# A four-layer gated transformer on one core: the order of VectorE and ScalarE in the first expert stage, single top-k rounds, ternary weights in three parts

## The chip, the core and the metric

The kernel runs on one core of a Trainium2 chip. A core has a matrix engine (TensorE), a vector engine (VectorE), a scalar engine with activation functions (ScalarE), a general engine (GpSimd), and SyncE, which here only issues transfers. Each engine executes its own instructions in program order and waits on semaphores for the others. Operands lie in SBUF (128 partitions); matrix products land in PSUM, eight banks of 128 x 512 fp32. The metric is device time in microseconds (us) of one execution; lower is better.

## The reference

The input x has 4 sequences of 256 tokens of width 256 (1024 tokens, eight tiles of 128). Four layers follow, each an attention-like block over a context `ctx` (4 x 256 x 64) and a feed-forward block, each added to x with a gate. What matters here:

```python
# layer 0: softmax of a normalized similarity, then a dense mixture of experts
x = x + tanh(g_xattn[0]) * L0_attention(layernorm(x), ctx)
logits = xn @ gate_w + gate_b;  top_idx = top_k(logits, 2)
all_out = relu(einsum('nsd,edo->nseo', xn, expert_w) + expert_b)   # 8 experts
x = x + tanh(g_ffn[0]) * take(all_out, top_idx).mean(axis=2)
# layer 1: causal attention with 16 heads, then a ternary feed-forward block
x = x + tanh(g_xattn[1]) * L1_attention(layernorm(x), ctx)
wq = clip(round(w / mean|w|), -1, 1) * mean|w|      # for w_gate, w_up, w_down
x = x + tanh(g_ffn[1]) * h_bitlinear(silu(bitlinear(xn, w_gate)) * bitlinear(xn, w_up), w_down)
# layer 2: a graph of ctx alone: rows of sim keep their 76 largest entries
sim = scores(ctx, ctx);  thr = top_k(sim, 76)[..., -1:]
A = sigmoid(sim) * (sim >= thr);  A = (A + A.T) / 2
```

Layers 2 and 3 end with routed experts. The graph A depends on ctx only and is needed first after layer 1.

## The kernel before

Everything is fp32 except a few bf16 operands. The work goes through stages one after the other; each has its own pool of PSUM banks. From the start to the end of layer 1's attention there are eight single banks, handed out in turn by `bank()`. A bank is free again when its last reader is done, so a late reader holds up the TensorE instruction that wants its bank.

The program is written as if in one sequence. A planner then places the instructions on the engines by its own model of time, except where `in_order(engine)` is entered: there the engine keeps the written order. TensorE is in written order from the kernel's first projections to the end of layer 1's attention. ScalarE is in written order up to `act_order.close()` (L778). VectorE is in written order only inside layer 0's attention (the `with` over pool `l0a`), and other VectorE work that is ready may still be placed among it.

Layer 0's attention (L568 to L674): `similarities(h, tiles)` transposes four normalized tiles, projects and squares; `softmax0` and `add0` finish the half. `graph_projections` and `graph_scores` compute `sim` for the graph between them (tile `gsim`, eight rows of tiles). `evac` copies PSUM to SBUF on VectorE (L109) and ScalarE (L111) in turn. `layernorm(h)` takes statistics of four tiles on VectorE (L167, L168), a power on GpSimd (L172) and a scaling on VectorE (L176).

Layer 0's experts (L717 to L778): `experts_of(h, xt)` routes four tiles (L195 with `router`) and picks two experts per token (`top2`: L215 to L221, coefficients `r_cw` L728, L729). `dense(t, ...)` runs one tile through all eight experts: four banks, each with a bias matmul (L736) and two matmuls of 128x512 (L741) for two experts; ScalarE applies Relu with the coefficient per expert (L748, tile `re`); GpSimd adds four experts to one in two steps (L753); VectorE adds the result to x (L361, two times per tile). `keys1` (L519) and `values1` (L534), one each in tiles 0 to 3, make layer 1's keys `kT` (L527 on VectorE, L529 on ScalarE) and values `va`. `ternary(n, raw)` quantizes one of three weights: sums of absolute values on ScalarE (L550), a matmul with ones that sums over partitions (L554), mean and reciprocal on VectorE (L556 to L558), scale on ScalarE (L560), clip on VectorE (L561), rounding on ScalarE (L562).

`graph_rows(t)` finds the 76th largest entry of each row by rounds: MAX8 gives eight largest (L485), MATCH_REPLACE8 (with a MATCH_VALUE_LOAD) strikes them out (L488). Ten rounds make a row tile, of which the last has no replacement but the selection L491. `ffn_tile(t)` is `dense(t)` and `graph_rows(t)`.

Layer 1's attention (L786 to L979) is a loop of 25 steps, four groups of heads for each of four sequences. In a step `Maxima.score(j)` writes masked scores to four banks (L803, L829, L834) and VectorE takes their maxima (L840, then L845, L846); one step later `late` transposes them (L852) and adds them to the queries (L855). `Maxima(b, xt)` projects the queries of one sequence (four products L195 with tile `wq`, evacuated to `qT`). `Sums`, four steps behind, computes exponentials on ScalarE (L880) and weighted sums (L888, L893), turns (L909, L925) and the output product. Steps 0 and 1 also run dense tiles 6 and 7, step 2 the third `ternary`, and steps 4 and 5 `graph_batch`, which symmetrizes the graph (transposes L500, add L505).

At the start the ScalarE queue issues the transfers of ctxT, of `cw` in two parts and of `bk`; SyncE's queue issues the eight x tiles, small vectors, the expert weights and later weights. Weights lie in a pool of ten tiles (`weights`, L115).

Of the kernel before, what the change touches and what calls it, by code (L numbers as in the profile page):

```python
# [27 lines left out]
P = 128  # L28
# [5 lines left out]
E = 8  # L34
# [31 lines left out]
def flamingo(ctx: ExitStack, tc: tile.TileContext, a: dict, out: bass.AP):  # L66
# [51 lines left out]


# [6 lines left out]
    nc.scalar.dma_start(cw[:, CW_K1:], a["cw"][:, CW_K1:])  # L126
# [13 lines left out]
    nc.sync.dma_start(gam, a["gamma_raw"].partition_broadcast(P))  # L140
    router = const.tile([P, KC, 3 * E + 1], F32, tag="router", name="router")
# [291 lines left out]
    in_l1 = ctx.enter_context(ExitStack())  # L433
    l1 = in_l1.enter_context(tc.tile_pool(name="l1", bufs=1))
    graph = const.tile([P, NT, S], F32, tag="graph", name="graph")
    until_l1 = ctx.enter_context(ExitStack())
    until_l1.enter_context(in_order())
    kv1 = until_l1.enter_context(tc.tile_pool(name="kv1", bufs=1))
# [18 lines left out]
    qkT2 = kv1.tile([P, 2, 2, S], F32, tag="qkT2", name="qkT2")  # L457

    def graph_projections():
        for side, c0 in enumerate((CW_Q2, CW_K2)):  # L460
            pk = bank()
            for i in range(2):
                nc.tensor.matmul(
                    pk[half(i), :], cw[half(i), c0 : c0 + C], ctxT[half(i)].rearrange("c h s -> c (h s)"),
                    start=True, stop=True,
                )
            evac(qkT2[:, side].rearrange("c h s -> c (h s)"), pk)

    def graph_scores(h):
# [11 lines left out]
    def graph_rows(t):  # L481
        left = gsim[:, t, :]
        for k in range(0, TOPK2, 8):
            m8 = sm([8], "g_m8")
            nc.vector.max(out=m8, in_=left)  # L485
            if k + 8 < TOPK2:
                work = kv1.tile([P, S], F32, tag="g_work", name="g_work", bufs=3)
                nc.vector.match_replace(out=work, in_to_replace=m8, in_values=left, imm_value=LOWEST)  # L488
                left = work
        last = (TOPK2 - 1) % 8  # L490
        nc.vector.scalar_tensor_tensor(  # L491
            graph[:, t, :], gsim[:, t, :], m8[:, last : last + 1], graph[:, t, :], ALU.is_ge, ALU.mult
        )
# [15 lines left out]
    vw = H1 * (D1 + 1)  # L509
    va = kv1.tile([P, NT, H1, 32], F32, tag="va1", name="va1")  # L510
# [36 lines left out]
    def ternary(n, raw):  # L547
        wsum = sm([2], "w_sum")
        for j in range(2):
            nc.scalar.activation(  # L550
                wq1[n][:, j * FF1 : (j + 1) * FF1], raw[j], AF.Abs, accum_out=wsum[:, j : j + 1]
            )
# [6 lines left out]
        for j, w in enumerate(raw):  # L559
            nc.scalar.activation(w, w, AF.Copy, bias=ROUND, scale=r)  # L560
            nc.vector.tensor_scalar(w, w, ROUND - 1.0, ROUND + 1.0, ALU.max, ALU.min)  # L561
            nc.scalar.activation(wq1[n][:, j * FF1 : (j + 1) * FF1], w, AF.Copy, bias=-ROUND)  # L562
# [5 lines left out]
    act_order = ExitStack()  # L568
    act_order.enter_context(in_order(ACT))
    with tc.tile_pool(name="l0a", bufs=1) as lp, in_order(mybir.EngineType.DVE):  # L570
# [93 lines left out]
        graph_projections()  # L664
# [4 lines left out]
        graph_scores(0)  # L669
        graph_scores(1)  # L670
# [3 lines left out]
        tiles1 = layernorm(1)  # L674
# [44 lines left out]
    if True:  # L719
        def experts_of(h, xt):  # L720

            pl = route(xt, 0, E)
            lg = sm([HT, E], "r_lg")
            nc.vector.tensor_add(lg, pl, rbias[:, 0:1, :].to_broadcast([P, HT, E]))
            hot = sm([2, HT, E], "top_hot")
            top2(lg, hot)
            half = sm([HT, E], "r_cw")
            nc.vector.tensor_add(half, hot[:, 0], hot[:, 1])  # L728
            nc.vector.tensor_scalar_mul(half, half, 0.5)  # L729
            return xt, half  # L730

        def dense(t, xt, half):
            i = t % HT
            pes = [bank() for _ in range(E // 2)]
            for j, pe in enumerate(pes):
                nc.tensor.matmul(  # L736
                    pe, onesb[32 * j : 32 * j + 3, :], eb[32 * j : 32 * j + 3, :], start=True, stop=False
                )
            for j, pe in enumerate(pes):
                for kc in range(KC):  # L740
                    nc.tensor.matmul(  # L741
                        pe, xt[:, kc, i * P : (i + 1) * P], ws0[j][:, kc * 2 * D : (kc + 1) * 2 * D],
                        start=False, stop=kc == KC - 1,
                    )
                if j % 2 == 0:
                    re = l0f.tile([P, 4, D], F32, tag="re", name="re")
                for e in (2 * j, 2 * j + 1):
                    nc.scalar.activation(  # L748
                        re[:, e % 4, :], pe[:, (e % 2) * D : (e % 2 + 1) * D], AF.Relu, scale=half[:, i, e : e + 1]
                    )  # L750
                if j % 2:
                    for n in (2, 1):
                        nc.gpsimd.tensor_add(re[:, :n, :], re[:, :n, :], re[:, n : 2 * n, :])  # L753
                    add_scaled(t, re[:, 0, :], gate(1, 0))

        chosen = experts_of(0, xt0)
        nc.scalar.activation(
# [713 lines left out]
```

## Time and profile before

| | us |
|---|---|
| median of 3 runs (831.25 to 832.45) | 832.28 |
| the profiled execution | 841.77 |
| its span, first to last instruction | 840.1 |
| TensorE busy in the span | 707.9 (84%) |
| VectorE busy | 509.9 (61%) |
| ScalarE busy | 283.8 (34%) |
| GpSimd busy | 208.6 (25%) |

The profile is of one execution. Busy means executing; a TensorE that runs at half of its clock counts as busy too, so the granted clock is given beside it. The page cuts the span into 40 slices of 21 us. Each digit is the busy share of a slice in tenths, and PEclk is the granted TensorE clock in tenths:

```profile
PE   3778837979998599639979998799999979979996
PEld 2434314556755376525557746645544335547754
DVE  6786998686674799764304445897777534213334
ACT  1442454333334234113103310146554655013320
POOL 4122321300001343110733452300000010733334
PEclk9868977989999899868989999899998998989999
```

PE is TensorE, PEld its loading of weights, DVE VectorE, ACT ScalarE, POOL GpSimd. Slices 0 and 1 hold layer 0's attention, slices 2 to 7 its experts, slices 8 to 12 layer 1's attention, slices 12 to 17 its feed-forward block; the other half belongs to layers 2 and 3.

A row of the timeline gives start, duration, engine, line, operation, output and inputs, shapes and count, and in brackets the idle time of the engine just before it and what ended that.

### The profile page before, as it was taken

To read this page: it belongs to the slowest core of one execution; us is meant where nothing else is said; L and a number is where in the kernel's file an instruction comes from. 1 tells how busy PE (TensorE), PEld (TensorE's weight loads), DVE (VectorE), ACT (ScalarE), POOL (GpSimd) and SP (SyncE) were. 2 spreads that over 40 slices of the span, in tenths; PEclk is the share of its full clock that TensorE was granted. 3 is DMA by queue.
4 is the path that set the end of the run, shared out by engine and by line. 5 is a ranking of instruction groups with operands and counts; after the bars stand their busy time and mean duration, and the time that the engine had idled before them with its cause. 6 is when DMAs were issued, how large, how long until landed. Compare 5 with 4: busy or idle time off the path is not lost.

```text
span 840.1 us, 11396 instructions
## 1 busy us (share of the span) xinstructions
PE 707.9 (84%) x4121; PEld 428.6 (51%) x4121; DVE 509.9 (61%) x1406; ACT 283.8 (34%) x583; POOL 208.6 (25%) x246
## 2 busy tenths in 40 slices
PE   3778837979998599639979998799999979979996
PEld 2434314556755376525557746645544335547754
DVE  6786998686674799764304445897777534213334
ACT  1442454333334234113103310146554655013320
POOL 4122321300001343110733452300000010733334
PEclk9868977989999899868989999899998998989999
DMA  7700011210000000000246932300000000369933
GB/s 229 272 0 1 0 38 38 75 39 1 21 2 20 1 1 1 0 1 0 101 150 225 320 89 79 128 1 2 1 1 2 1 1 0 116 225 330 332 114 107
DMA packets 32848, 64.35 MB, mean 77 GB/s; under 512 B 5180, under 2 KB 22488, under 8 KB 32536
## 3 DMA queue, kind: packets, MB, share of 16 engines
q0 software_dynamic: 8224, 31.76, 11.3%
q1 hardware_dynamic: 23992, 31.08, 11.2%
q10 hardware_dynamic: 576, 0.79, 0.3%
q8 instruction: 33, 0.54, 0.3%
q14 instruction: 23, 0.19, 0.1%
HBM read 49.31 MB, written 14.30 MB: 76 GB/s over the span
## 4 chain that ended last, share of the span: by engine, by line
PE 53%; DVE 20%; issue 12%; ACT 5%; DMA 5%; POOL 3%; another core or an unknown queue 2%; SPq 0%; ACTq 0%; DVEq 0%; POOLq 0%
PE b L195 20%; PE b L741 5%; PE b L388 5%; PE b L1235 4%; PE b L1204 3%; PE b L1250 3%; PE b L1051 3%; DVE pad L1211 3%; DVE x L361 3%; DMA d_w<-in_ffn_r_dram,d_of 3%; PE b L336 3%; DVE g_m L485 2%; DVE g_work L488 2%; ACT pT L1242 1%
## 5 line engine op out<-in xcount | busy, mean ns | idle before, releaser
L195 PE MATMUL b<-xnT,w 128*128 128x512 f32 (+2 forms) x288 | 122.1, 582 | 5.9 <-DVE xnT L109 5.5
L1211 DVE TENSOR_REDUCE pad<-b 128x2 f32<-128x512 f32 x128 | 81.0, 685 | 20.1 <-PE b L1235 19.4
L195 PEld LDWEIGHTS b<-xnT,w 128*128 128x128 f32 (+1 forms) x288 | 57.1, 203 | 63.2 <-issue 53.1
L1242 ACT ACTIVATE pT<-b 128x512 f32<-128x512 f32 x128 | 68.7, 598 | 50.8 <-PE b L1235 50.8
L1204 PE MATMUL b<-kT,qT 32*128 32x256 f32 x512 | 72.4, 419 | 3.2 <-DVE pad L1211 3.2
L1235 PE MATMUL b<-qm,kT 32*128 32x512 f32 x256 | 73.7, 650 | 0.0
L301 POOL DMA_INDIRECT d_w<-in_ffn_r_dram,d_of x46 | 43.8, 953 | 120.3 <-PE b L308 71.2
L741 PE MATMUL b<-w,xnT 128*128 128x512 f32 x128 | 66.0, 675 | 0.0
L388 PE MATMUL b<-w,hT 128*128 128x256 f32 x224 | 55.2, 397 | 8.1 <-issue 4.8
L195 PE MATMUL b<-d_w,d_xT 128*128 128x256 f32 (+1 forms) x184 | 57.1, 433 | 4.9 <-ACT d_xT L111 2.4
L1204 PEld LDWEIGHTS b<-kT,qT 32*128 32x128 f32 x512 | 42.2, 192 | 32.8 <-DVE pad L1211 10.8
L373 ACT ACTIVATE sil<-b 128x512 f32<-128x512 f32 (+1 forms) x28 | 16.6, 597 | 119.8 <-PE b L195 77.1
L388 PEld LDWEIGHTS b<-w,hT 128*128 128x128 f32 x224 | 42.2, 195 | 22.1 <-issue 13.5
L753 POOL TENSOR_TENSOR re<-re 128x512 f32<-128x512 f32 (+1 forms) x32 | 32.2, 1009 | 68.5 <-ACT re L748 67.2
L172 POOL TENSOR_TENSOR ln_rstd<-ln_ve,neghalf 128x4 f32<-128x4 f32 x16 | 16.3, 1019 | 126.8 <-DVE ln_ve L170 120.2
L374 DVE TENSOR_TENSOR hT<-b,sil 128x512 f32<-128x512 f32 (+1 forms) x28 | 19.3, 689 | 44.1 <-ACT sil L373 41.1
L741 PEld LDWEIGHTS b<-w,xnT 128*128 128x128 f32 x128 | 27.1, 218 | 34.9 <-issue 34.9
L1051 PE MATMUL b<-had,zT 128*128 128x256 f32 x128 | 34.6, 429 | 10.5 <-ACT hwork L1062 7.2
L880 ACT ACTIVATE pT<-b 128x384 f32<-128x384 f32 x64 | 26.2, 495 | 45.4 <-PE b L874 45.4
L353 POOL DMA_INDIRECT d_yt<-rows_out,d_row x32 | 31.1, 972 | 33.5 <-DMA rows_out<-d_y 24.3
L748 ACT ACTIVATE re<-b,r_cw 128x256 f32<-128x256 f32 x64 | 26.1, 475 | 38.9 <-PE b L741 22.6
L195 PEld LDWEIGHTS b<-d_w,d_xT 128*128 128x128 f32 x184 | 32.0, 194 | 13.8 <-ACT d_xT L111 3.1
(277 smaller groups left out, 1301.0 us busy)
## 6 DMA issues: line engine op xcount, KB each, us to landing
d_x<-rows_in SPq DMA_DIRECT2D x46, 128.0 KB
rows_out<-d_y SPq DMA_DIRECT2D x46, 128.0 KB
w<-in_ffn_s_dram SPq DMA_DIRECT2D x13, 384.0 KB
w<-in_l_w_dram SPq DMA_DIRECT2D x6, 512.0 KB
rows_in<-zero SPq DMA_DIRECT2D x1, 2944.0 KB
w<-in_expert_w_dram SPq DMA_DIRECT2D x4, 512.0 KB
x<-in_x_dram SPq DMA_DIRECT2D x8, 128.0 KB
kT<-in_l_kT_dram SPq DMA_DIRECT2D x1, 1024.0 KB
```

The source lines that it names most:

```text
L195: nc.tensor.matmul(dst, lhs(kc), rhs(kc), start=kc == 0, stop=kc == KC - 1)
L301: nc.gpsimd.indirect_dma_start(out=w, out_offset=None, in_=src, in_offset=self.indices(self.of[:, n : n + 1]))
L353: nc.gpsimd.indirect_dma_start(out=y, out_offset=None, in_=rows_out, in_offset=self.indices(self.at[:, n, t : t + 1]))
L388: nc.tensor.matmul(po, hT[:hs, j, i * P : (i + 1) * P], w[:hs, 4 * hs : 4 * hs + D], start=j == 0, stop=j == len(ws) - 1,)
L741: nc.tensor.matmul(pe, xt[:, kc, i * P : (i + 1) * P], ws0[j][:, kc * 2 * D : (kc + 1) * 2 * D], start=False, stop=kc == KC - 1,)
L753: nc.gpsimd.tensor_add(re[:, :n, :], re[:, :n, :], re[:, n : 2 * n, :])
L880: nc.scalar.activation(self.pT[:, n, :], pn[n][:, : 3 * P], AF.Exp, scale=0.25)
L1051: nc.tensor.matmul(pf[:, c // 2, (c % 2) * 2 * P : (c % 2 + 1) * 2 * P], self.zT[:, c0 : c0 + P], had2[:, n].rearrange("p s q -> p (s q)") ...
L1204: nc.tensor.matmul(pn[:, half * S : (half + 1) * S], self.qT[group(k), ah, g0 + half, qt * P : (qt + 1) * P], kT[group(k), ah, self.b * S ...
L1211: nc.vector.tensor_reduce(self.pads[qt][:, ah, g0 : g0 + 2, k, D3], pn.rearrange("p (g s) -> p g s", g=2), AX.X, ALU.max, negate=True,)
L1235: nc.tensor.matmul(pn, kT[group(k), ah, c : c + P], self.qm[group(k), ah, g0 : g0 + 2, :], start=True, stop=True)
L1242: nc.scalar.activation(self.pT[u][:, k, :], pn, AF.Exp, scale=D3**-0.5)
```

## The change

- GpSimd's memset of `va` is written at the kernel's very beginning. It fills only the 15 of 32 columns that no value is written to, and the column of ones, where before the whole tile was filled. For this the pools `l1` and `kv1` are opened first.
- The second part of `cw` is issued on SyncE's queue, after `gam` and ahead of `router`, and no longer on ScalarE's.
- VectorE and ScalarE are both in written order from layer 0's attention to the end of dense tile 5 (`all_orders`). The second `layernorm(1)` is written after the choice of experts for the first half; the Sigmoid of the graph is written after dense tile 0; `layernorm(0)` for layer 1 is written in tile 4.
- `dense` adds all eight experts on GpSimd (a third add per tile), and `add_mean` adds them to x once per tile, one tile later. Tile `re` has three buffers.
- `graph_rows(n)` advances a generator by n rounds. Tiles 0 to 5 take 5, 6, 7, 7, 4 and 5 rounds, in two portions each; each attention step takes three until none is left. `graph_batch` is written in steps 20 to 23.
- `ternary` is split in `ternary_mean`, `ternary_scale` and `ternary_round`. For the first weights they are written in tiles 1, 2, 3, for the second in tiles 3, 4, 5, for the third all in step 2.
- `qkT2` lies in the pool of layer 0's attention.

```diff
+    in_l1 = ctx.enter_context(ExitStack())
+    l1 = in_l1.enter_context(tc.tile_pool(name="l1", bufs=1))
+    until_l1 = ctx.enter_context(ExitStack())
+    kv1 = until_l1.enter_context(tc.tile_pool(name="kv1", bufs=1))
+    va = kv1.tile([P, NT, H1, 32], F32, tag="va1", name="va1")
+    nc.gpsimd.memset(va[:, :, :, D1 + 1 :], 0.0)
+    nc.gpsimd.memset(va[:, :, :, D1 : D1 + 1], 1.0)
...
-    nc.scalar.dma_start(cw[:, CW_K1:], a["cw"][:, CW_K1:])
...
     nc.sync.dma_start(gam, a["gamma_raw"].partition_broadcast(P))
+    nc.sync.dma_start(cw[:, CW_K1:], a["cw"][:, CW_K1:])
...
-    def graph_rows(t):
-        left = gsim[:, t, :]
-        for k in range(0, TOPK2, 8):
...
+    def graph_rounds():
+        for t in range(NT):
+            left = gsim[:, t, :]
+            for k in range(0, TOPK2, 8):
+                m8 = sm([8], "g_m8")
+                nc.vector.max(out=m8, in_=left)
+                if k + 8 < TOPK2:
+                    work = kv1.tile([P, S], F32, tag="g_work", name="g_work", bufs=3)
+                    nc.vector.match_replace(out=work, in_to_replace=m8, in_values=left, imm_value=LOWEST)
+                    left = work
+                    yield
...
+            yield
+    rounds = graph_rounds()
+    def graph_rows(n):
+        for _ in range(n):
+            next(rounds, None)
...
-    act_order = ExitStack()
-    act_order.enter_context(in_order(ACT))
-    with tc.tile_pool(name="l0a", bufs=1) as lp, in_order(mybir.EngineType.DVE):
+    all_orders = ExitStack()
+    all_orders.enter_context(in_order(ACT))
+    all_orders.enter_context(in_order(mybir.EngineType.DVE))
+    with tc.tile_pool(name="l0a", bufs=1) as lp:
...
         add0(1, *weighted)
-        tiles1 = layernorm(1)
...
-                if j % 2:
-                    for n in (2, 1):
-                        nc.gpsimd.tensor_add(re[:, :n, :], re[:, :n, :], re[:, n : 2 * n, :])
-                    add_scaled(t, re[:, 0, :], gate(1, 0))
...
+            if j % 2:
+                for n in (2, 1):
+                    nc.gpsimd.tensor_add(re[:, :n, :], re[:, :n, :], re[:, n : 2 * n, :])
+        nc.gpsimd.tensor_add(means[0][:, 0, :], means[0][:, 0, :], means[1][:, 0, :])
+        return means[0][:, 0, :]
...
+    counts0 = choose(route(xt0, 0, E))
+    tiles1 = layernorm(1)
...
+    for t in range(NT - 2):
+        if t == 1:
+            pl = route(xt1, 0, E)
+        means[t] = dense(t % HT, *((xt0, counts0) if t < HT else (xt1, counts1)))
+        if t == 0:
+            nc.scalar.activation(
+                graph.rearrange("p t s -> p (t s)"), gsim.rearrange("p t s -> p (t s)"), AF.Sigmoid,
+                scale=1.0 / 16.0,
+            )
+        graph_rows(3)
+        if t == 1:
+            counts1 = choose(pl)
+        if t:
+            add_mean(t - 1)
+        if t == 4:
+            tiles = layernorm(0)
+        graph_rows((2, 3, 4, 4, 1, 2)[t])
+        if t == 0:
+            xt1 = transposed(tiles1)
+        if t < HT:
+            keys1(t)
+            values1(*divmod(t, 2))
+        for n in range(2):
+            if t == 1 + 2 * n:
+                ternary_mean(n)
+            if t == 2 + 2 * n:
+                ternary_scale(n)
+            if t == 3 + 2 * n:
+                ternary_round(n)
+    all_orders.close()
...
-            xt = transposed(layernorm(0))
+            xt = transposed(tiles)
...
                 if n < 2:
-                    ffn_tile(NT - 2 + n)
+                    means[6 + n] = dense(2 + n, xt1, counts1)
+                    add_mean(5 + n)
                 elif n == 2:
+                    add_mean(7)
                     in_l0f.close()
-                    ternary(2, raw[2])
-                elif n in (4, 5):
-                    graph_batch(2 * n - 8)
-                    graph_batch(2 * n - 7)
+                    ternary_mean(2)
+                    ternary_scale(2)
+                    ternary_round(2)
+                elif steps <= n < steps + B:
+                    graph_batch(n - steps)
...
                     todo()
+                graph_rows(3)
```

## The prediction

> **What bounds the kernel now.** I read the 40 slices first (21 us each), then stretches of 10 us, then the waits between 45 and 180 us, then the timeline. The dense stage of layer 0 and the first attention steps (50 to 200 us) have the worst TensorE rows. Stretches; columns are TensorE, its weight loads, VectorE, ScalarE, GpSimd (busy us, count), granted clock, DMA share, GB/s:
>
> ```profile
> 100.00:110.00 10.00, 8.12 (x20) 3.76 (x21) 9.55 (x31) 1.83 (x4) 0.73 (x1) 0.83 0.00 1
> 110.00:120.00 10.00, 1.31 (x4) 0.24 (x2) 9.08 (x33) 4.66 (x6) 1.02 (x1) 0.80 0.15 52
> 120.00:130.00 10.00, 5.32 (x12) 2.48 (x13) 9.16 (x31) 7.85 (x17) 4.01 (x4) 0.51 0.10 26
> 130.00:140.00 10.00, 5.73 (x20) 2.81 (x18) 9.14 (x27) 6.55 (x12) 2.93 (x3) 1.00 0.28 79
> 140.00:150.00 10.00, 8.78 (x25) 6.08 (x26) 7.41 (x24) 0.74 (x2) 1.07 (x2) 0.66 0.01 2
> ```
>
> VectorE works nine tenths of the time while TensorE has holes: VectorE's top-k stands ahead of small operations that others wait for. The waits (who for whom: us in total, times, longest):
>
> ```profile
> ACT w L560 <- DVE rmw L558: 17.4, 3, 11.4
> PE b L554 <- ACT wq L550: 16.1, 2, 13.4
> PE b L195 <- DVE xnT L109: 15.1, 3, 6.8
> DVE x L361 <- POOL re L753: 11.3, 8, 3.0
> ```
>
> ScalarE waited 11.4 us for a reciprocal queued behind top-k rounds; TensorE's mean matmul (L554) stands behind that ScalarE work, hence the 13.4 us hole. TensorE's holes between 62 and 141 us, from the timeline: 2.8 (xnT), 2.7 and 13.4 (L554), 5.5 (xnT): 24.4 us. From 200 us on the steps run at TensorE's pace (4.35 us each) with VectorE half idle.
>
> **The change, part by part.** Positions are those of the profiled run before (span 840.1).
>
> *Early memset, cw on another queue.* From the timeline:
>
> ```profile
> 12.10 3.50 POOL L767 MEMSET va<- 128x4096 f32 x1
> 12.76 2.92 DVE L445 CAST eb<-ebias 16x128 bf16<-16x128 f32 x1
> ```
>
> The cast's two other executions took 0.20 us; it was held until the memset ended, and the chain of waits runs through it. The new memset comes before VectorE's first instruction (3.54) and fills 15 of 32 columns (about 1.7 us from the row above), so ident comes 2 us later, with its first use at 10.54. That frees 2.9 us, but ebias, which landed at 12.73, becomes the limit: SyncE issues one DMA more ahead of it (0.43 each), so it lands at 13.2. From the cast's end to the xnT copy's end are 2.8 us: 16.2 instead of 18.45, a gain of **2.2**. Ends: 0.5 (ebias also waits for the 384 KB moved ahead of it) and 3.5 (x tiles land earlier without that transfer beside them).
>
> *No rounds in the second softmax.* VectorE's order is now by hand to the end of dense tile 5, so the nine top-k instructions at 39.4 to 47.6 go. Without them the copies of gsim end at 40.0, the reductions at 43.6, the exponentials at 45.2, ScalarE's xnT copy at 45.8 (was 48.2): the route, and dense(0), start **2.4** earlier, at 48.9.
>
> *Dense tiles 0 to 5.* choose() now runs without layernorm(1) and rounds between its operations, so the Relus start near 52 (were 57.9); TensorE did not wait for them. In the built order TensorE's mean matmuls stand after tiles 1 and 3; before, they stood ahead of tiles 4 and 5. TensorE in order, durations from the trace:
> dense(0) 10.8, transposes 1.1, keys and values 1.6: 62.3. Route waits for ScalarE: last Relu 60.5, table load 1.28, the Sigmoid now behind dense(0) 1.91, xnT copy 0.59: 64.3 (hole 2.0). Route 2.7, dense(1) 10.0: 77.0. Keys 1.5, then two Abs behind the kT and va copies: 81.25 (hole 2.7, the same queue as before tile 4). dense(2) 9.4, keys 1.5, dense(3) 7.5, keys 1.5: 101.2. The second mean waits for two rounding copies (L562, 2.0) and two Abs (2.1): 106.0 (hole 4.8, where 13.4 was). dense(4) 9.4, dense(5) 7.5, transposes 1.1: 124.0. xnT: ScalarE has its last Relu at 123.8, two rounding copies 2.0, copy 0.6: 126.4; VectorE, last held by the clip of tile 4's weights to 119.3, has 6.5 rounds, an add and a bn_stats (7.1), copy 0.6: 127.0. So the q projections start at 127.0 (were 141.2), **14.2** earlier: holes 12.5 for 24.4, and the 2.4 above.
>
> The clock: after a hole of 2.7 us the trace has
>
> ```profile
> 101.88 0.38 PE L554 MATMUL b<-w_sum,ones 128*128 128x2 f32 x2 [2.68 <-ACT wq L550]
> 102.54 8.77 PE L741 MATMUL b<-w,xnT 128*128 128x512 f32 x16
> ```
>
> against 7.13 for the same sixteen without a hole (90.57). [...] I take the row[...].
>
> *Rounds that move.* 34 of the 80 rounds stay in tiles 0 to 5; before, 68 MAX8 were done by 141. The other 46 are written three to a step, but VectorE is not in hand order there, and in the built order all 46 stand ahead of the eighth step's reductions. From the xnT copy to that point VectorE has 46 MAX8 (0.47 from start to next start), 41 replaces (0.52), 5 selects (0.45), 28 reductions L840 (1.87 per four), nine copies 3.7, layernorm, adds, clips and small ones 9: **71 us**. Check: that stretch before is 58.8 us with 41.4 busy; 33 MAX8, 30 replaces, 3 selects more are 32.5, two adds and four graph_batch adds fewer 3.6: 70.3.
>
> ```profile
> 39.40:141.20 101.80, 70.28 (x214) 34.15 (x212) 88.81 (x308) 45.33 (x90) 27.75 (x29) 0.81 0.05 16
> 141.20:200.00 58.80, 53.68 (x386) 34.07 (x390) 41.39 (x122) 19.71 (x40) 9.08 (x9) 0.89 0.14 41
> ```
>
> TensorE reaches score(0) at 142.5, score(1) at 151.5, VectorE their reductions at 145.1 and 157.8: VectorE is the bound, with perhaps 1 us of waits. 127.0 + 71 + 1 = 199, against 200.0: of 14.2 us won, **0.9** is left. This is the main point: the rounds taken out of the dense stage come back in steps that had 17 us of VectorE idle and receive 29 us net.
>
> *Adds.* Sixteen adds to x become eight (0.48 each); GpSimd gets a third add per tile (0.75). [...] Row: one x add beside GpSimd took 1.50 us at 95.28. [...] MAX8 ranges only from 396 to 431 ns whatever GpSimd does, and is what stands beside them: I take 0, end +2. The adds now come a tile late, so the 11.3 us of waiting for GpSimd goes; its time is in the walk.
>
> *graph_batch* moves to steps 20 to 23: 4 x 0.5 us of TensorE in the drain, where TensorE waits 0.62, 0.68 and 0.57 for others (262 to 267), and 0.6 of VectorE each, beside 3.8 idle: **+0.5** (0 to 2). The third weights' Abs is now placed before tile 4's Relus (105.9 to 108.1), whose first bank is ready at 108.5; its second load waits for the first weights' rounding (about 103) instead of 116.25, and those 512 KB landed inside the slice that issued them: 0. The expert weights are issued 0.43 later; all early loads are in by 40 (DMA share 0.00 from there), dense(0) starts after 46: 0.
>
> Sum: -2.2 - 0.9 + 0.5 = **-2.6**: span 837.5. The profiled execution took 841.77 with its ends, the median is 832.28; I take the difference off the median: **829.7**.
>
> **Rivals.** *The clock stays up in short holes* [...]: dense stage 4 us shorter, with the x tiles early 1 more: about 824.5. For: 2.0 and 2.7 us are the shortest holes in this stage[...]; against: the 8.77. *Reductions ping-pong* (slower): in-order VectorE does 10 to 12 rounds ahead of each L840, holding four of eight PSUM banks; TensorE then starts the next score late, cold, and VectorE waits in turn. Where VectorE idles over 4.3 us in steps 0 to 7, the change is slower; 1.5 us in each of six steps is +9: about 838. For: TensorE's wait for L840 at 174.32 already exists; against: my walk has 3 us of slack at most steps. *Nothing arrives*: ebias lands late (0.5 gained), the drain costs 1, the steps eat the rest: 832.
>
> **Chances.** Forecast 0.45 (827 to 832.5), clock rival 0.25, ping-pong 0.20, nothing 0.10. A difference below 0.2% (1.7 us) can't be told from no change. Faster: 0.32 + 0.25 + 0.01 = 0.58; same: 0.12 + 0.01 + 0.09 = 0.22; slower: 0.01 + 0.19 = 0.20. Range 823.5 to 836.5.
>
> **What would show it.** xnT copy of layer 0 near 16; dense(0) near 46.5; holes of about 2.7 and 4.8 before the mean matmuls, none of 13; first q projection near 125; VectorE over 95% busy from there for 70 us, TensorE near 0.75; eighth step's L840 near 197. Wrong if that VectorE stretch is much under 70 us, if TensorE alternates with it, or if dense(1) and dense(2) take 7.1.

## The result, and the profile after

The kernel after takes 821.53 us (median of 4 runs, 818.73 to 823.86), the kernel before 832.37 (4 runs, 831.25 to 832.59). The ratio is 0.9871, 95% interval 0.9838 to 0.9904: 10.8 us faster, where 2.6 were forecast. The profiled execution of after took 823.86 us with a span of 822.1.

The two profiled spans differ by 18.0 us, more than the medians. The landmarks tell why. The columns give starts in us; the last one is the difference.

| landmark (TensorE, if nothing else is said) | before | after | earlier |
|---|---|---|---|
| VectorE's xnT copy of layer 0 (L109) | 17.78 | 15.30 | 2.5 |
| first bias matmul of dense(0) (L736, after L752) | 51.35 | 46.69 | 4.7 |
| first q projection of layer 1 (L195, after L204) | 141.22 | 121.89 | 19.3 |
| VectorE's reductions of the eighth step (L840, after L874) | 200.03 | 188.98 | 11.1 |
| first transposes of layer 1's feed-forward block (L1006, after L1044) | 269.32 | 258.99 | 10.3 |
| first expert-shared down projection (L388, after L397) | 414.26 | 404.13 | 10.1 |
| first transpose of routed tokens (L308, after L317) | 443.12 | 424.81 | 18.3 |

So the change has its whole gain, 10.3 us, at the start of layer 1's feed-forward block. The last 8 us come from a stall in the one profiled execution of before. It is treated as the first experiment.

The early part, from the timeline of after; columns are start, duration, engine, line, operation, output and inputs, shapes, count, and the wait:

```profile
0.81 1.70 POOL L124 MEMSET va<- 128x1920 f32 x1 [0.29 <-POOLq L1499]
...
12.97 0.21 DVE L450 CAST eb<-ebias 16x128 bf16<-16x128 f32 x1 [1.39 <-DMA ebias<-in_expert_b_dram]
...
15.30 0.67 DVE L109 COPY xnT<-b 128x512 f32<-128x512 f32 x1
```

The cast is back at its own 0.21 us and now waits for its transfer, as the prediction had it. TensorE in the dense stage of after, the same view:

```profile
47.23 9.18 PE L758 MATMUL b<-w,xnT 128*128 128x512 f32 x16
...
59.83 0.36 PE L204 MATMUL b<-router,xnT 128*128 128x8 f32 x2 [1.05 <-DVE xnT L109]
61.04 2.65 PE L204 MATMUL b<-router,xnT 128*128 128x8 f32 x14 [0.85 <-ACT xnT L111]
...
77.59 0.38 PE L565 MATMUL b<-w_sum,ones 128*128 128x2 f32 x2 [2.69 <-ACT wq L561]
...
78.23 8.83 PE L758 MATMUL b<-w,xnT 128*128 128x512 f32 x16
...
88.81 7.13 PE L758 MATMUL b<-w,xnT 128*128 128x512 f32 x16
...
102.00 0.38 PE L565 MATMUL b<-w_sum,ones 128*128 128x2 f32 x2 [4.57 <-ACT wq L561]
...
102.65 8.78 PE L758 MATMUL b<-w,xnT 128*128 128x512 f32 x16
...
121.89 5.38 PE L204 MATMUL b<-xnT,w 128*128 128x256 f32 x16 [2.19 <-ACT wq L578]
```

The brackets hold the holes: 1.9, 2.7, 4.6 and 2.2 us, where before had 2.8, 2.7, 13.4 and 5.5. The sixteen matmuls take 7.13 us where none precedes them and 8.8 behind one (those of dense(0), at 47.23, stand behind the route and its wait of 5.1 us for xnT). In the waits of after between 45 and 180 us (who for whom: us in total, times, longest), VectorE's wait for GpSimd's `re` is gone, and TensorE's wait at the means and ScalarE's for the reciprocal have shrunk, from 16.1 and 17.4 us:

```profile
PE b L565 <- ACT wq L561: 7.3, 2, 4.6
...
ACT w L573 <- DVE rmw L569: 3.6, 1, 3.6
```

Now the stretches. The columns are length, then busy us of TensorE, its weight loads, VectorE, ScalarE and GpSimd, the granted clock, DMA share and GB/s. First after, from dense(0) to the q projections, and from there to the eighth step's reductions:

```profile
46.69:121.90 75.21, 63.86 (x190) 29.28 (x189) 55.72 (x191) 41.80 (x80) 31.36 (x31) 0.88 0.04 12
121.90:188.98 67.08, 55.98 (x370) 34.33 (x374) 63.87 (x210) 19.93 (x41) 11.26 (x12) 0.82 0.15 47
```

In the second stretch VectorE works 95% of the time, as forecast. Before and after over the whole way from dense(0) to the eighth step, one line from each trace:

```profile
51.35:200.03 148.68, 119.26 (x575) 63.88 (x578) 119.51 (x395) 58.69 (x119) 35.26 (x35) 0.85 0.09 27
```

```profile
46.69:188.98 142.29, 119.84 (x559) 63.61 (x562) 119.59 (x400) 61.73 (x120) 42.62 (x43) 0.85 0.09 28
```

VectorE is busy for the same 119.5 us, but it does 80 MAX8 in that time where it did 74. Its idle time falls from 29.2 to 22.7 us, by as much as the stretch gets shorter. Part of the reason is in the groups of these stretches (columns: busy us and mean ns of one, then idle time ahead and what ended it), before and after:

```profile
L361 DVE SCALAR_TENSOR_TENSOR x<-re,gates,x 128x256 f32<-128x256 f32 x16 | 11.1, 694 | 11.3 <-POOL re L753 11.3
```

```profile
L370 DVE SCALAR_TENSOR_TENSOR x<-re,gates,x 128x256 f32<-128x256 f32 x8 | 4.2, 526 | 0.0
```

Sixteen adds with 11.3 us of waiting became eight without any: 6.9 us of work and 11.3 us of waits less. Other waits of VectorE grew in turn, as its idle time fell by only 6.5 us.

### The profile page after: what moved, and what is told of

Read it like the earlier page. It is cut to its first block, busy times and chain, and to the rows that moved or that the text cites. A ratio compares the mean times of both kernels' runs of the same rounds, so it can differ in the third digit from the quotient of the medians.

```text
span 822.1 us, 11367 instructions
## 1 busy us (share of the span) xinstructions
PE 706.4 (86%) x4115; PEld 428.4 (52%) x4121; DVE 505.3 (61%) x1398; ACT 283.9 (35%) x583; POOL 213.9 (26%) x254
## 4 chain that ended last, share of the span: by engine, by line
PE 53%; DVE 18%; issue 12%; DMA 7%; ACT 5%; POOL 5%; SPq 0%; DVEq 0%; POOLq 0%; ACTq 0%
PE b L204 18%; PE b L758 6%; PE b L397 5%; PE b L1273 4%; PE b L1288 3%; PE b L1242 3%; PE b L1089 3%; DMA d_w<-in_ffn_r_dram,d_of 3%; DVE pad L1249 3%; PE b L345 3%; DVE x L370 2%; POOL rows_in L295 2%; ACT pT L1280 1%; DVE g_work L493 1%; DVE g_m L490 1%
## 5 line engine op out<-in xcount | busy, mean ns | idle before, releaser
L204 PE MATMUL b<-xnT,w 128*128 128x512 f32 (+2 forms) x288 | 121.1, 578 | 8.0 <-DVE m L874 3.3
L1249 DVE TENSOR_REDUCE pad<-b 128x2 f32<-128x512 f32 x128 | 80.9, 684 | 20.7 <-PE b L1273 20.2
L204 PEld LDWEIGHTS b<-xnT,w 128*128 128x128 f32 (+1 forms) x288 | 56.4, 200 | 64.3 <-issue 54.8
L204 PE MATMUL b<-d_w,d_xT 128*128 128x256 f32 (+1 forms) x184 | 57.8, 438 | 4.8 <-DMA d_w<-in_ffn_r_dram,d_of 3.9
L397 PE MATMUL b<-w,hT 128*128 128x256 f32 x224 | 53.9, 396 | 2.0 <-DVE hT L383 2.0
L397 PEld LDWEIGHTS b<-w,hT 128*128 128x128 f32 x224 | 42.3, 195 | 15.0 <-issue 6.9
L383 DVE TENSOR_TENSOR hT<-b,sil 128x512 f32<-128x512 f32 (+1 forms) x28 | 19.3, 689 | 46.0 <-ACT sil L382 46.0
L204 PEld LDWEIGHTS b<-d_w,d_xT 128*128 128x128 f32 x184 | 32.5, 196 | 13.3 <-ACT d_xT L111 4.2
```

Of the source, the lines that this page charges most:

```text
L204: nc.tensor.matmul(dst, lhs(kc), rhs(kc), start=kc == 0, stop=kc == KC - 1)
L397: nc.tensor.matmul(po, hT[:hs, j, i * P : (i + 1) * P], w[:hs, 4 * hs : 4 * hs + D], start=j == 0, stop=j == len(ws) - 1,)
L1249: nc.vector.tensor_reduce(self.pads[qt][:, ah, g0 : g0 + 2, k, D3], pn.rearrange("p (g s) -> p g s", g=2), AX.X, ALU.max, negate=True,)
```

## The experiments

The experiments ran in four groups, each on one chip with runs of the kernel before beside them; these took 849.1, 843.5, 831.8 and 830.5 us. So ratios to before are compared, and from the profiles the start of dense(0) and the *stretch* from there to the first transposes of layer 1's feed-forward block. Repeats of one kernel differ by 0.3 us (before) and 0.9 us (after) in the stretch, and by 0.3 and 1.2 us in the start of dense(0).

| kernel | time | ratio to before (95%) | dense(0) | q proj. | stretch |
|---|---|---|---|---|---|
| before, first profile | 832.37 | | 51.35 | 141.22 | 218.0 |
| before_again | 850.62 | one execution | 51.68 | 141.82 | 218.3 |
| after, first profile | 821.53 | 0.9871 (0.9838 to 0.9904) | 46.69 | 121.89 | 212.3 |
| after_again | 833.98 | 0.9886 (0.9852 to 0.9920) | 47.84 | 123.93 | 213.2 |
| early_alone | 845.51 | 0.9959 (0.9941 to 0.9977) | 48.65 | 138.35 | 218.0 |
| early_means | 825.54 | 0.9940 (0.9915 to 0.9964) | 48.57 | 135.69 | 214.8 |
| ternary_whole | 833.16 | 0.9890 (0.9846 to 0.9934) | 47.72 | 120.94 | 212.3 |
| rows_whole | 837.01 | 0.9894 (0.9845 to 0.9944) | 47.29 | 134.17 | 218.1 |
| order_open | 820.49 | 0.9874 (0.9850 to 0.9898) | 49.03 | 133.64 | 209.9 |
| open_adds_back | 822.34 | 0.9908 (0.9876 to 0.9941) | 48.20 | 135.47 | 215.4 |
| no_step_rounds | 826.11 | 0.9718 (0.9691 to 0.9746) | 47.74 | 123.32 | 200.9 |
| two_chains | 836.07 | 0.9854 (0.9829 to 0.9878) | 47.75 | 123.60 | 212.4 |
| mean_later | 833.12 | 0.9870 (0.9831 to 0.9909) | 47.42 | 118.30 | 212.2 |
| both | 815.38 | 0.9796 (0.9757 to 0.9835) | 46.73 | 115.50 | 205.8 |
| open_two_mean | 811.09 | 0.9753 (0.9724 to 0.9782) | 48.36 | 123.12 | 202.1 |
| spread | 836.55 | 1.0049 (1.0029 to 1.0069) | 47.13 | 121.83 | 228.2 |
| spread_two | 826.67 | 0.9943 (0.9923 to 0.9963) | 47.76 | 122.80 | 219.4 |
| spread_two_mean | 817.49 | 0.9833 (0.9808 to 0.9859) | 47.70 | 116.34 | 212.8 |

**Is the stall of 8 us part of the change?** Both kernels were profiled again, unchanged.

> The kernel before, unchanged, profiled once more. Theory 1 (the change gains only up to the start of layer 1's FFN, 10.3 us; the other 7.8 us between the two profiled spans are a stall of that one execution of before, whose TensorE stood idle 4.5 us in layer 1's expert-shared matmuls L388 and ran cold after it): no such idle time here, span near 831, first L1006 transposes again near 269.3. Theory 2 (the kernel before has that stall by its nature and the change removes it): the stall is there again, span near 840.

> The kernel after, unchanged, beside its relatives on one chip. In the two first profiles the stretch from the first expert-shared down projection of layer 1 (L397) to the first transposes of d_x took 28.9 us before and 20.7 after, TensorE waiting 4.5 us there for nothing that the profile names while GpSimd's gathers of d_w moved 360 to 400 GB/s. Theory 1 (this stall comes and goes between executions and chips and is not the change): here it takes about 28.7 as in all other runs, and layer 1's FFN starts at 259 to 260. Theory 2 (the change removes it): 20.7 again.

In the stretch from the down projections to the first routed tokens, before_again took 28.7 us and after_again 28.2 (28.9 and 20.7 in the first profiles). The rows of before_again, from the timeline:

```profile
414.97 11.90 PE L388 MATMUL b<-w,hT 128*128 128x256 f32 x54
428.64 0.38 PE L388 MATMUL b<-w,hT 128*128 128x256 f32 x1 [1.77 <-issue]
430.06 0.38 PE L388 MATMUL b<-w,hT 128*128 128x256 f32 x1 [1.05 <-issue]
432.16 4.05 PE L388 MATMUL b<-w,hT 128*128 128x256 f32 x8 [1.72 <-issue]
```

Single matmuls stand between waits that nothing in the profile ends ("issue"), 4.5 us in all. All eight profiles of the first two groups had this stall, after and its relatives among them; the eight of the last two groups had none (20.7 us each). It goes with the chip or the execution and not with the change: theory 2 falls, and so does the part of theory 1 that expected no stall in before_again. The gain to explain is the 10.3 us ahead of it.

**What does the early memset give alone?**

```diff
+    va = kv1.tile([P, NT, H1, 32], F32, tag="va1", name="va1")
+    nc.gpsimd.memset(va[:, :, :, D1 + 1 :], 0.0)
+    nc.gpsimd.memset(va[:, :, :, D1 : D1 + 1], 1.0)
...
-    nc.scalar.dma_start(cw[:, CW_K1:], a["cw"][:, CW_K1:])
...
+    nc.sync.dma_start(cw[:, CW_K1:], a["cw"][:, CW_K1:])
```

> Before, with the early memset of va and the moved part of cw alone. Theory 1: layer 0's xnT copy ends 2.5 us earlier (17.8 to 18.5 becomes 15.3 to 16.0), TensorE's bias matmuls (first L736) start 2.3 earlier, and since everything after runs in the same order, the time falls by about 2.3 us (0.28%), to about 830.0. Rival: the dense stage waits for VectorE's top-k and not for the route, so the 2.3 us are lost there: below 0.5 us.

The ratio 0.9959 is 3.5 us of 849.1 (interval 2.0 to 5.0). dense(0) starts 3.0 us earlier than in before_again, the stretch behind it is unchanged (218.0). Nothing is lost later: the rival falls, and the gain is more than the 2.3 us of theory 1.

**Does the split of the ternary weights pay?**

```diff
         for n in range(2):
-            if t == 1 + 2 * n:
+            if t == 3 + n:
                 ternary_mean(n)
-            if t == 2 + 2 * n:
                 ternary_scale(n)
-            if t == 3 + 2 * n:
                 ternary_round(n)
```

> After, with the ternary weights in one piece again (mean, scale and rounding together after tiles 3 and 4, as before), all else as after. Theory 1 (the split shortens the second hole from 13.4 to 4.6 us because ScalarE no longer waits for a reciprocal in the same tile): the hole ahead of the second mean grows to 8 to 13 us, the q projections start 4 to 9 us later, time 4 to 8 us above after. Rival (VectorE's order by hand shortened it, with the rounds counted out per tile, whatever the split): holes together within 2 us of after's 7.3, time within 2 us.

The holes ahead of the means are 2.7 and 3.0 us, shorter together than after's 7.3, and the stretch is 212.3. The rival holds: beside VectorE's order by hand the split is worth nothing. Two runs further down complete this. order_open has the split and not that order, and its holes are 2.7 and 4.6 us; early_means has neither, and its second hole is 12.3 us. So either of the two shortens it. With either, ScalarE no longer waits long for the reciprocal: 6.7 us in all in ternary_whole and 2.7 in order_open, where it was 17.4 in before and 16.9 in early_means.

**Does it matter who places the rounds, and where?** In rows_whole each dense tile takes ten rounds again, by hand (seven behind the three that are written first):

```diff
-        graph_rows((2, 3, 4, 4, 1, 2)[t])
+        graph_rows(7)
...
+                    graph_rows(10)
...
-                graph_rows(3)
```

In order_open VectorE's order by hand ends with layer 0's attention:

```diff
         add0(1, *weighted)
+        dve_order.close()
```

> After, with all ten rounds of a tile of the graph in each dense tile (60 in tiles 0 to 5, 20 in the first two steps), all else as after. Theory 1 (VectorE's rounds cost about 0.98 us wherever VectorE is the bound, and in tiles 0 to 5 it was idle only some 17 us): 26 more rounds are 25 us, the q projections start 6 to 12 us later, the steps get 8 to 10 us shorter, time within 4 us of after. Rival (single rounds between the steps are what gains): time over 8 us above after, near before.

> After, with VectorE's order by hand ending with layer 0's attention, as before, so that the planner places the rounds in and behind the dense stage. Measured by the stretch from dense(0)'s first bias matmul to layer 1's first L1044 transposes: 218.0 and 218.3 us before, 212.3 and 213.2 after. Theory 1 (what gained is that fewer rounds stand in the dense stage, whoever puts them there, and the planner pulls them all forward): the q projections start at 130 to 140, the stretch is 216 to 220, as before. Rival (the order by hand is only a detail): 212 to 214.

With whole row tiles by hand the stretch is 218.1 us, as before the change: the copy of xnT stands behind ten rounds, and the route to the second half waits 5.75 us for it. Theory 1 allowed a loss of 4 us in time, its rival gave over 8. By time it is 3.0 us, with intervals that overlap; in the stretch it is 5 to 6, between the two. order_open goes against theory 1 altogether: the planner does pull the rounds forward (63 of the MAX8 on `g_work` run between 30 us and the q projections, 31 in after), the projections start at 133.64, and still the stretch is 209.9. dense(0) starts later there, at 49.03, and the sum, layer 1 at 258.9, is that of after (259.0 and 261.1). So, with the rest of the change in place, the order by hand is not what gains; the planner does as well. By hand, with whole row tiles, it is worse.

**Is VectorE the bound of the first steps?** no_step_rounds leaves out the rounds of the attention steps, so that its graph is not the right one.

```diff
-                graph_rows(3)
```

> After, with the top-k rounds of the attention steps left out: 46 of the 80 rounds are not computed, so rows of the graph from the fourth tile on keep all their values. Theory 1 (VectorE sets the pace from the first q projection to the eighth step: 67.3 us, 44 of them rounds): without them TensorE sets it; TensorE waited about 10 us for the reductions there and ran at a clock of 0.82; the eighth step's reductions come 10 to 15 us earlier (174 to 179 instead of 189), time 807 to 812. Rival (TensorE or ScalarE sets the pace and the rounds lie beside it): under 3 us gained.

The reductions of the eighth step come at 178.6, and layer 1's feed-forward block starts 10.4 us earlier than in after (12.5 than in after_again). The stretch is 200.9. Theory 1 holds: VectorE works 27.6 us from the q projections to that step, for 63.9 in after, and TensorE sets the pace (50.4 of 55.3 us). So the rounds in the steps cost 11 to 12 us of stretch.

**Can the bound be moved?** In two_chains the rounds of two row tiles alternate:

```diff
-        for t in range(NT):
+        for t in range(0, NT, 2):
+            pair = (t, t + 1)
...
+                for i, u in enumerate(pair):
+                    nc.vector.max(out=m8[i], in_=left[i])
+                yield
+                for i, u in enumerate(pair):
+                    if k + 8 < TOPK2:
...
```

In mean_later the mean matmul stands behind the next dense tile, and ScalarE's Abs stay; the kernel `both` has the two edits.

```diff
             if t == 1 + 2 * n:
-                ternary_mean(n)
+                ternary_abs(n)
             if t == 2 + 2 * n:
+                ternary_mean(n)
                 ternary_scale(n)
```

> After, with the rounds of two tiles alternating: two MAX8, then two MATCH_REPLACE8, so that most of these instructions do not read what the one just ahead of them wrote. In the trace of after a MAX8 that is followed by its own replace takes 0.46 us from start to start, the replace with its value load 0.52; where an instruction of something else stands between, 0.33 and 0.40. Theory 1 (VectorE is the bound in the first eight steps, and a dependent instruction waits for the end of the one ahead of it): 46 rounds times 0.2 are 9 us of VectorE; the eighth step's reductions come 5 to 9 us earlier, time 813 to 817. Rival (the start-to-start time is the instruction's own, or TensorE is the bound): within 1 us of after.

> After, with the mean of a ternary weight (TensorE's matmul over w_sum and the three small VectorE operations) moved behind the next dense tile, whereas ScalarE's Abs stay where they are. Theory 1 (TensorE's holes of 2.7 and 4.6 us ahead of these matmuls, and the cold dense tiles behind them, 8.8 instead of 7.1 us, are lost time): the dense stage is 8 to 10.6 us shorter, q projections near 112, time 4 to 9 us below after. Rival (VectorE is the bound of the whole stretch to the eighth step, so what TensorE gains VectorE's rounds take back): below 2 us.

> After, with the rounds of two tiles alternating and the means moved behind the next dense tile; VectorE's order in the attention steps is the planner's. Theory (VectorE is the bound of the dense stage; with late means TensorE's gain turned into a wait of 8.4 us for an xnT copy behind rounds; faster rounds bring that copy 6 us earlier): wait of 1 to 4 us, stretch 206 to 210. Rival: as each of the two alone, 212.

Each alone brings nothing in the stretch (212.4 and 212.2), against theory 1 in both cases. mean_later shows why. From its timeline, the dense tiles right behind the two means, and the q projections:

```profile
85.50 7.13 PE L763 MATMUL b<-w,xnT 128*128 128x512 f32 x16
...
101.89 7.13 PE L763 MATMUL b<-w,xnT 128*128 128x512 f32 x16
...
118.30 6.75 PE L204 MATMUL b<-xnT,w 128*128 128x256 f32 x16 [8.41 <-DVE xnT L109]
```

The holes are gone and the matmuls behind them run at 7.13 us. What TensorE gained has become a wait of 8.4 us for VectorE, whose xnT copy stands behind rounds. In two_chains a round costs 0.78 us, but theory 1 set this against the 0.98 of an unbroken chain. In after other work stands within many rounds, and on the way from the q projections to the eighth step a MAX8 takes 0.41 us and a replace with its load 0.48 from start to start, 0.90 a round. So VectorE's busy time on that way falls from 63.9 to 60.7 us, not by 9, and it stands idle for 5.9 us instead of 3.2. With both edits the stretch is 205.8: neither engine alone is the bound, and each edit waited for the other. The wait ahead of the q projections is still 6.3 us, for 1 to 4 expected.

**Do the rounds cost less if they are spread by hand?** VectorE's order by hand is held through the attention steps, with nine rounds in each of the first two and two in each later step.

```diff
-    all_orders.close()
+    act_order.close()
...
-                graph_rows(3)
+                graph_rows(9 if n < 2 else 2)
...
+        all_orders.close()
```

> After, with VectorE's order by hand held through the attention steps, nine rounds in each of the first two steps (beside their dense tiles) and two in each later one; so no twelve rounds stand ahead of a reduction. Same work. Theory 1 (VectorE is the bound up to the eighth step because all 46 rounds are placed ahead of its reductions; spread over 16 steps a step costs VectorE about 4.7 us, little over TensorE's 4.35): the stretch from dense(0) to layer 1 falls from 213 to 204 to 208 us, time 5 to 9 us below after. Rival (an order by hand makes VectorE wait for TensorE in each step, in turn with it): 213 or more.

> As the kernel with the rounds spread by hand, and the rounds of two tiles alternating (0.78 us a round in the run of two chains, for 0.98). Theory 1 (there the faster rounds brought nothing because the planner placed more of them ahead of the same reductions, and VectorE waited for TensorE in turn): a step costs VectorE 4.3 us, below TensorE's 4.35; the stretch is 200 to 204 us, near the 200.9 without any rounds in the steps. Rival: no shorter than with spreading alone.

> As the last, and the ternary means moved behind the next dense tile. Theory 1 (in the kernel with the late means TensorE's gain of 10 us became a wait of 8.4 us for an xnT copy queued behind rounds; with faster rounds VectorE is done earlier by 34 times 0.2 us): the wait ahead of the q projections shrinks to 1 to 3 us and the stretch falls by 4 to 8 us more, to 193 to 199. Rival (VectorE is still the bound of the dense stage): within 2 us of the last.

The rival holds for the first: the stretch is 228.2, and the kernel is slower than before. In written order the first step's rounds stand behind its reductions, so VectorE has nothing to do while TensorE runs dense tile 6. Then nine rounds stand ahead of two copies of q that TensorE's next scores need, and TensorE waits. One row from each engine's timeline:

```profile
136.39 1.95 DVE L875 TENSOR_REDUCE m<-b 128x3 f32<-128x384 f32 x4 [9.15 <-PE b L869]
...
159.43 1.17 PE L838 MATMUL b<-cmask,identb 128*128 128x256 bf16 x3 [7.32 <-DVE qT L109]
```

They also wait for each other later. From the waits of this kernel between 120 and 262 us:

```profile
DVE m L875 <- PE b L869: 12.8, 4, 9.2
...
PE b L838 <- DVE m L875: 9.3, 7, 3.4
```

Faster rounds and late means take 8.8 and 6.5 us off that (219.4, 212.8), but from a bad start: neither stretch is what theory 1 gave, and the wait ahead of the q projections is 6.1 us in the last, for 1 to 3 expected. This is the ping-pong that the prediction had as a rival, made by an order by hand. An order that spreads the rounds and puts them elsewhere within a step was not tried.

**Do the adds pay?** From both sides. In open_adds_back, order_open has 16 adds to x again:

```diff
-        nc.gpsimd.tensor_add(means[0][:, 0, :], means[0][:, 0, :], means[1][:, 0, :])
-        return means[0][:, 0, :]
...
+                add_scaled(t, re[:, 0, :], gate(1, 0))
```

In early_means, early_alone has eight:

```diff
-                    add_scaled(t, re[:, 0, :], gate(1, 0))
+            nc.gpsimd.tensor_add(means[0][:, 0, :], means[0][:, 0, :], means[1][:, 0, :])
+            add_scaled(t, means[0][:, 0, :], gate(1, 0))
```

> As the kernel with VectorE's order open (stretch from dense(0) to layer 1: 209.9 us), with the adds to x as before: one for each half of the experts, 16 instead of 8, right behind GpSimd's two adds, and no third GpSimd add. Theory 3 (the adds are what paid behind dense(0): before, 16 took 11.1 us of VectorE, 694 ns each, and VectorE waited 11.3 us for GpSimd ahead of them; after, 8 take 4.2 us and wait for nothing): the stretch grows by 4 to 8 us, to 214 to 218. Rival (they are small beside the rest, as the prediction priced them, 0.48 us each on VectorE and nothing for GpSimd): below 2 us.

> The kernel before with the early memset, and of all else only the merged add (a third GpSimd add per dense tile, one add to x instead of two; and the tile qkT2 in layer 0's pool, to make room for it). Theory 3: the stretch falls from the 218.0 us of the kernel with the early memset alone to 211 to 214, time 4 to 7 us below it. Rival: 216.5 to 218, as the holes of 13.4 us ahead of the second mean stay.

Taking the merged add back costs 5.5 us of stretch (209.9 to 215.4). The group of adds in order_open and in open_adds_back, from 47 to 190 us:

```profile
L370 DVE SCALAR_TENSOR_TENSOR x<-re,gates,x 128x256 f32<-128x256 f32 x8 | 3.8, 477 | 4.1 <-POOL re L774 4.1
```

```profile
L370 DVE SCALAR_TENSOR_TENSOR x<-re,gates,x 128x256 f32<-128x256 f32 x16 | 8.7, 544 | 12.0 <-POOL re L772 12.0
```

Adding it to early_alone gains 3.2 us (218.0 to 214.8), less than the 4 to 7 expected, with the hole ahead of the second mean still 12.3 us. Theory 3 is confirmed from the first side and in sign from the second: the merged add is worth 3 to 5.5 us of stretch, where the split and the order by hand, each taken back alone, were worth nothing. In the times the intervals of both pairs overlap (0.9850 to 0.9898 and 0.9876 to 0.9941; 0.9941 to 0.9977 and 0.9915 to 0.9964): the profiles carry it, one of each kernel.

**The best version.** open_two_mean is order_open with the alternating rounds and the late means:

> As the last, with VectorE's order left to the planner from the end of layer 0's attention on. Theory (the planner fills the dense stage with rounds, so that few are left for the steps; with order open alone the stretch was 209.9 and TensorE waited 10.6 us ahead of the q projections): wait below 5 us, stretch 201 to 207, the best of all, time 6 to 12 us below after. Rival (the planner puts faster rounds ahead of the same small operations): 209 to 211.

The stretch is 202.1 and the ratio 0.9753 (0.9724 to 0.9782), below after's interval in both of its measurements: 19.4 us below before, where after is 10.8. The wait ahead of the q projections is 8.3 us, not below 5 as expected; by then 68 of the 80 MAX8 are done (35 in after), and from there to the eighth step TensorE works 51.6 of 56.4 us and VectorE 38.0. By time it can't be told from `both` (0.9757 to 0.9835); the stretch is 3.7 us shorter.

## Why the prediction was wrong

The direction was right, and 8 us were missing. All of them lie behind dense(0): up to there the sum (2.2 and 2.4) gave 4.6 us and the first profile shows 4.7.

**Early memset, right.** The xnT copy was to end at 16.2 and ends at 15.97, held by ebias as forecast; alone the part gives 3.5 us by time and 3.0 by landmark, for 2.2.

**No rounds in the second softmax, right in the first profile and less in others.** 2.4 were forecast. Kernels with it start dense(0) at 46.7 to 47.8, early_alone at 48.65: 0.8 to 2.0.

**The dense walk, right in order and 3 us too long.** The holes were given as 2.0, 2.7, 4.8 and 3.0 and are 1.9, 2.7, 4.6 and 2.2. With the early part, the q projections were due at 124.8 and start at 121.9: dense(0) takes 9.6 us with its bias, for 10.8 (the granted clock is 0.50 for its first 4.7 us, where before it was for 6.7), the last hole is 0.8 shorter, and the other tiles are 0.1 to 0.4 shorter each. **The clock** was decided for the row, and rightly: behind the 2.69 us hole sixteen matmuls take 8.83 us, and 7.13 in mean_later, where the hole is taken away. The granted clock is 0.50 from 78.7 to 82.1 us, at the start of those matmuls, and 0.99 and 1.00 on its two sides; behind the 4.57 us hole it is 0.50 from 102.6 to 106.0. So each hole cost about 1.7 us of clock (8.83 and 8.78 us for 7.13). In open_two_mean three waits of 0.17, 0.36 and 0.36 us between the bias matmuls stand ahead of another 8.83 us.

**Rounds that move: the term that failed.** "46 MAX8 (0.47 from start to next start), 41 replaces (0.52), 5 selects (0.45)" make 45.2 us; in the trace of after, from start to next start without waits, 45 MAX8, 41 replaces with their loads and 5 selects take 40.6. The count was right and so was the rest of the sum (reductions 13.1, measured 13.0; all else 12.7, measured 12.4); the waits were 1.2 for 1. The price was that of rounds in an unbroken chain, 0.98 to 0.99 us; in after one took 0.90. From VectorE's timeline of after, six rows with other work between the parts of a round, and six of a chain:

```profile
140.68 0.41 DVE L490 MAX8 g_m<-g_work 128x8 f32<-128x256 f32 x1
141.02 0.40 DVE L176 BATCH_NORM_STATS2 ln_st<-x 128x6 f32<-128x256 f32 x1
141.35 0.07 DVE L493 MATCH_VALUE_LOAD g_work<-g_m,g_work 128x8 f32 x1
141.41 0.40 DVE L493 MATCH_REPLACE8 g_work<-g_m,g_work 128x256 f32<-128x256 f32 x1
141.73 0.16 DVE L177 BATCH_NORM_AGGREGATE ln_mv<-ln_st 128x2 f32<-128x6 f32 x1
141.84 0.43 DVE L490 MAX8 g_m<-g_work 128x8 f32<-128x256 f32 x1
142.31 0.09 DVE L493 MATCH_VALUE_LOAD g_work<-g_m,g_work 128x8 f32 x1
142.38 0.41 DVE L493 MATCH_REPLACE8 g_work<-g_m,g_work 128x256 f32<-128x256 f32 x1
142.83 0.43 DVE L490 MAX8 g_m<-g_work 128x8 f32<-128x256 f32 x1
143.29 0.09 DVE L493 MATCH_VALUE_LOAD g_work<-g_m,g_work 128x8 f32 x1
143.37 0.41 DVE L493 MATCH_REPLACE8 g_work<-g_m,g_work 128x256 f32<-128x256 f32 x1
143.81 0.43 DVE L490 MAX8 g_m<-g_work 128x8 f32<-128x256 f32 x1
```

In the chain a MAX8 comes 0.45 us after its replace has begun, and the next load 0.46 after the MAX8. Where the next instruction does not need the result, it begins after 0.32 to 0.34 us, ahead of the recorded end of the one before. So the stretch took 67.3 us and not 72, and of the 19.3 us won 11.1 were left, not 3.1. Of these 8 us 3 come from the dense walk and 4.6 from this price.

**Adds: no part of the 8 us, but priced too low by themselves.** The prediction took 0 for them and left the 11.3 us of waits to the walk. The walk and the price of the rounds make up 7.6 of the 8 us, so the adds are not a further miss of the sum. As a part of the change they are worth 3 to 5.5 us, which the prediction did not say. Its price of 0.48 us is that of an undisturbed add: twelve of the sixteen took 0.46 to 0.49 us, four took 0.93 to 1.50, each begun while a GpSimd add ran. Of the 6.9 us of work saved, the eight adds fewer are 3.8 and these overlaps 3.1. GpSimd's adds also have a cost in after: four xn scalings (L185) took 1.38 us at 52.91, nearly all of it ahead of GpSimd's first adds, and 2.80 at 109.65 beside two of them. That is 1.4 us, inside the bound of +2 that was kept.

**graph_batch in the drain.** +0.5 was forecast; from the eighth step to layer 1's end the gain falls from 11.05 to 10.33, 0.7. It was not tried alone.

**The rivals.** The clock did not stay up: it is 0.50 behind the hole of 2.7 us as behind that of 4.6. No trace of before had shown that it would behind such a hole. The ping-pong did not come: VectorE idled 3.2 us from the q projections to the eighth step, below the 4.3 from which it was to decide; spread shows it. "Nothing arrives" fell with the first landmark.

What stays open: how the 5.7 us behind dense(0) divide between the merged add and the four symmetrizing adds moved out of the way (2.6 us of VectorE). Moving these was not tried alone, nor were the split and the order by hand taken back together.

## What to carry to other kernels

Price an instruction by what stands ahead of it: among VectorE instructions of 0.41 us here, one that needs the previous result came 0.46 us after it and one that does not 0.33, so a round took 0.90 us with other work between its links and 0.98 in an unbroken chain. Where the schedule already puts other work there, the rest of the gain is small (VectorE's busy time fell by 3.2 us here, for 9 forecast). Where two engines bound a stage in turn, an edit that helps one can show nothing until the other is helped too; try such edits together before dropping them. Two parts of a change can also stand in for each other, so that taking back either alone costs nothing. Taking small adds and their waits off the busiest engine was worth more here than either of those two.

## What was unexpected of the hardware

- In the rows of after above, VectorE begins an independent instruction before the recorded end of the previous one (0.32 to 0.34 us from start to start for 0.40 to 0.41 us each). A load that needs the MAX8 ahead of it, or a MAX8 that needs the replace ahead of it, begins after that end (0.45 to 0.47 us from start to start). A round took 0.78 us in alternating chains, for 0.98 in one.
- The four slow adds of before began 0.05 to 0.08 us after a GpSimd add and ended 0.28 to 0.29 us after that one's end (95.28 to 96.78 us beside 95.23 to 96.50), as if they had waited for it.
- TensorE stood still for 3.8 to 5.1 us in all at one place without any releaser, and lost 8 us with the slow matmuls behind it. It came in before's first profile and in all eight of the first two groups, and neither in after's first nor in the eight of the other two. GpSimd's gathers kept the DMA engines busy meanwhile (before, 426.4 to 431.5 us: share 1.02, 342 GB/s), but in after they do the same (416 to 422 us: 1.00, 338 GB/s) and TensorE works throughout (6.00 of 6.00 us). What it waits for, no run shows.
